# A graph-attention layer on one Trainium2 core: three late scores in one exponential, scores in batches of three and five, first loads spread

## The chip, the cores and the metric

The kernel runs on one core of a Trainium2 chip. The metric is the device time of one launch in microseconds. The engines are named as the profile names them: PE (matrix products, with PEld for its weight loads), DVE (vector), ACT (activation functions), POOL (GpSimd) and SP, whose queue issues most of the DMAs.

## The reference, cut to what matters

The network has four layers on 3327 nodes with 128 features and a dense 0/1 adjacency matrix. Each layer adds its output to x. Layer 1, an attention with 128 heads of size 8, takes nearly all the time, and all of the change is in it:

```python
h = jnp.maximum(_layernorm(x, axis=-1), 0.0)
q = (h @ Wq.T).reshape(d, n, 8)        # d = 128 heads, n = 3327 nodes
k = (h @ Wk.T).reshape(d, n, 8)
v = (h @ Wv.T).reshape(d, n, 8)
a = jnp.einsum('dnh,dmh->dnm', q, k) * d ** (-0.5)
a = a + adj + adj                       # twice the adjacency, the same for all heads
a = jax.nn.softmax(a, axis=2)
out = jnp.einsum('dnm,dmh->dnh', a, v).reshape(n, 8 * d) @ Wo.T
```

So for every head there is a 3327 x 3327 matrix of scores; twice the adjacency is added, the exponential is taken, and the result weighs the values. A ninth value column of ones gives the sum for the softmax.

## The kernel before, in words

Layer 0 runs first. Then comes a start stage (L458 to L478): for each of 26 row tiles r, PE makes q, k and v, ACT copies them out of PSUM (L466, L474), and SP stores them to DRAM (L440). Beside this, a list `early` (L444 to L457) holds pieces of other work, one of which is taken after each row: splitting q and k of the first groups into a high and a low part on POOL (`Parting`, L356), the loads of the first group (`load_heads`, L392), and rounding its keys (`key_pair`, L414). The exponentials of the adjacency for the first query chunk (`exp_of`, L345) are listed there too, though the program places them ahead of this stage on ACT. SP's queue runs in order, so a load that waits holds up the stores listed behind it.

The attention loop (L578 to L624) is written out by hand, and each engine takes its instructions in that order. There are 7 chunks of queries (six of 476 columns and one of 471, computed as 472), 32 groups of four heads, and 26 key tiles of 128 keys: 224 groups, and 2912 pairs of key tiles. One step is one key tile for four heads.

`scores` (L536) makes four products of a step, one head in each group of 32 rows of PE's array. Each of them ends up exponentiated in one of eight places of the tile `p8`, which a pair of steps shares. There are three ways, named in `WAYS` (L505):

- "D": the score goes to a one-bank PSUM tile `early` (four buffers), DVE adds the doubled adjacency `a2` (L552), and at the end of the pair one exponential on ACT covers the five D places (L557).
- "I": the score goes to a tile `late`, PE itself adds the doubled adjacency with the matrix `two_i` (L550), and ACT takes the exponential (L553).
- "G": the score goes to `late`, ACT takes the exponential (L553), and POOL multiplies by the exponential of the adjacency (L555).

An even step has D, D, D, I, an odd one D, D, I, G. So a pair has two L553 exponentials, of one score from a one-bank `late1` and of two scores from a two-bank `late2`, and one L557 of five scores. `weigh` (L559) multiplies the places of a step with the values and sums over the 26 key tiles in one PSUM bank `acc`; it runs four steps behind the scores. At a group's end DVE copies `acc` to `o4` (L573), and the next group's first values must wait for that copy. [...]

Of the kernel before, what the change touches and what calls it, by code (L numbers as in the profile page):

```python
# [8 lines left out]
F32 = mybir.dt.float32  # L9
# [6 lines left out]
AF = mybir.ActivationFunctionType  # L16
# [5 lines left out]
P = 128  # L22
# [32 lines left out]
def kernel(  # L55
# [285 lines left out]
    def even(c):  # L341
        w = q_chunks[c][1]
        return w + w % 2
# [45 lines left out]
                if t == 11:  # L389
                    self.store(side)  # L390

    def load_heads(c, g):  # L392
        q0, w = q_chunks[c]
        k_in = kq.tile([P, NP], F32, name="k_in", bufs=1)
        q4 = kq.tile([P, QW], F32R, name="q4")
        v4 = kq.tile([P, 4, T, EA], F32, name="v4")
        nc.gpsimd.memset(k_in[:, N:], 0.0)
        if w % 2:
            nc.gpsimd.memset(q4[:, w : w + 1].bitcast(F32), 0.0)
        for i in range(4):  # L400
            n0 = (4 * g + i) * N
            for j in range(2):
                r = 32 * i + HL * j
                nc.sync.dma_start(k_in[r : r + HL, :N], kt[:, n0 : n0 + N])
                nc.sync.dma_start(q4[r : r + HL, :w].bitcast(F32), dram(qt, E * j * GP + n0 + q0, [[0, 2], [GP, E], [1, w]]))
        for i in range(4):
            n0 = (4 * g + i) * N
            nc.sync.dma_start(
                v4[:, i].rearrange("p t e -> p (t e)"),
                vd[n0 : n0 + NP, :].rearrange("(p t) e -> p (t e)", t=T),  # L410
            )
        return k_in, q4, v4, []

    def key_pair(heads):  # L414
# [7 lines left out]
    with tc.tile_pool(name="l1", bufs=1) as pool, tc.tile_pool(name="l1_ps", bufs=3, space=PSUM) as ps:  # L422
        w_st = pool.tile([D, 3, NH * E], F32, name="w_st")
        for i, w in enumerate((wq, wk, wv)):
            nc.gpsimd.dma_start(w_st[:, i, :], w)
        zero = pool.tile([HL, NH], F32, name="zero")
        nc.vector.memset(zero, 0.0)
        nc.gpsimd.dma_start(vd[N * NH : N * NH + 1, :], zero[:1, :EA])
        for end in (qf, kf):
            nc.gpsimd.dma_start(end[:E, N * NH :], zero[:E])  # L430

        with tc.tile_pool(name="l1_ln", bufs=1) as ln, tc.tile_pool(name="l1_tp", bufs=2, space=PSUM) as tps:
            h, done = layernorm_relu(ln)
            done(T)
            hT = transposed(pool, tps, h, "hT")
        st = ctx_st.enter_context(tc.tile_pool(name="l1_st", bufs=4))

        def store(dst, src, r, kp):
            for p0, p1 in ((0, kp),) if kp == P else ((0, 112), (112, kp)):
                nc.sync.dma_start(dst[r * P + p0 : r * P + p1], src[p0:p1])  # L440


        assert 7 * N + NP <= 2 * P * NH
        early = []  # L444
        for g in range(2):
            part = Parting(g)
            for side in range(2):
                early.append(lambda part=part: (part.load(0), part.load(1)) if part.lo[0] is None else None)
                early.append(lambda part=part, side=side: [part.part(side, i) for i in range(4)] and part.store(side))
        first, e_first = [], []  # L450
        early.append(lambda: first.extend(load_heads(0, 0)))
        ahead_part = Parting(2)
        early.append(lambda: (ahead_part.load(0), ahead_part.load(1)))
        early.append(lambda: e_first.extend(exp_of(a, 0) for a in a_first[1::2]))
        early += [lambda: (key_pair(first), key_pair(first))] * (T // 4)
        if T // 2 % 2:
            early.append(lambda: key_pair(first))  # L457
        for r in range(T):  # L458
            kp = rows_of(r)
            lhs = hT[:, r * P : r * P + kp]  # L460
            for i, (dst, mx) in enumerate(((qf, q_max), (kf, k_max))):
                pp = ps.tile([P, 2, 512], F32, name="pp", bufs=2)
                for c in range(2):
                    nc.tensor.matmul(pp[:kp, c, :], lhs, w_st[:, i, c * 512 : c * 512 + 512], start=True, stop=True)
                s = st.tile([P, E * NH], F32, name="qk_st")
                nc.scalar.activation(s[:kp], pp[:kp].rearrange("p a b -> p (a b)"), AF.Copy, scale=D**-0.5 if i == 0 else 1.0)  # L466
                nc.vector.tensor_reduce(mx[:kp, r : r + 1], s[:kp], AX.X, ALU.max, apply_absolute_value=True)
                store(dst[:E].rearrange("e (r c) -> r e c", c=NH), s.rearrange("p (e c) -> p e c", c=NH), r, kp)
            pp = ps.tile([P, 2, 512], F32, name="pp", bufs=2)
            for c in range(2):  # L470
                nc.tensor.matmul(pp[:kp, c, :], lhs, w_st[:, 2, c * 512 : c * 512 + 512], start=True, stop=True)
            s = st.tile([P, NH, EA], F32, name="v_st")
            nc.gpsimd.memset(s[:, :, E : E + 1], 1.0)
            nc.scalar.copy(s[:kp, :, :E], pp[:kp].rearrange("p a (c e) -> p (a c) e", e=E))  # L474
            store(vd.rearrange("(r c) e -> r (c e)", c=NH), s.rearrange("p c e -> p (c e)"), r, kp)

            if r > 1 and early:
                early.pop(0)()  # L478
        while early:
            early.pop(0)()  # L480

        mx4 = pool.tile([P, 4], F32, name="mx4")
        for i, m in enumerate((q_max, k_max, a_max, low_bits)):
            nc.vector.tensor_reduce(mx4[:, i : i + 1], m, AX.X, ALU.max)
        all4 = pool.tile([P, 4], F32, name="all4")
        nc.gpsimd.partition_all_reduce(all4, mx4, P, bass_isa.ReduceOp.max)
        bound = pool.tile([P, 1], F32, name="bound")
        nc.vector.tensor_mul(bound, all4[:, 0:1], all4[:, 1:2])  # L490
        nc.vector.tensor_scalar_mul(bound, bound, 1.01 * E / 2)
        nc.vector.tensor_add(bound, bound, all4[:, 2:3])
        fits = pool.tile([P, 2], F32, name="fits")
        nc.vector.tensor_scalar(fits[:, 0:1], bound, SAFE / 2, None, op0=ALU.is_le)
        nc.vector.tensor_scalar(fits[:, 1:2], all4[:, 3:4], 0.0, None, op0=ALU.is_equal)
        nc.vector.tensor_mul(unsafe, fits[:, 0:1], fits[:, 1:2])
        nc.vector.tensor_scalar(unsafe, unsafe, -1.0, 1.0, op0=ALU.mult, op1=ALU.add)
        ctx_st.close()
# [3 lines left out]

    WAYS = ("DDDI", "DDIG")  # L505
    PLACES = ((0, 1, 2, 5), (3, 4, 6, 7))
    two_i = const.tile([P, P], BF16, name="two_i")
    nc.vector.tensor_copy(two_i, ident)
    engines = {
# [9 lines left out]
    with tc.tile_pool(name="at_in", bufs=1) as a_pool, tc.tile_pool(name="at_p", bufs=3) as p_pool, tc.tile_pool(  # L519
# [13 lines left out]
            q0, w = q_chunks[c]  # L533
            nc.sync.dma_start(adj16[t][:, q0 : q0 + w], a2[:, :w])

        def scores(step, heads, a2, e_a, p8):  # L536
            c, _, t = step
            we = even(c)
            _, q4, _, pairs = heads
            ways, places = WAYS[t % 2], PLACES[t % 2]  # L540
            n_d = ways.count("D")
            late = ps.tile([P, 4 - n_d, 512], F32, name=f"late{4 - n_d}")
            early = [ps.tile([P, 512], F32, name="early", bufs=4) for _ in range(n_d)]
            for i in (*range(n_d, 4), *range(n_d)):
                r = slice(32 * i, 32 * i + 32)
                sp = early[i] if i < n_d else late[:, i - n_d]
                nc.tensor.matmul(sp[:, :we], pairs[t // 2][r, t % 2, :], q4[r, :we], start=True, stop=ways[i] != "I")  # L547
            for i in range(4):
                if ways[i] == "I":
                    nc.tensor.matmul(late[:, i - n_d, :we], two_i, a2[:, :we], start=False, stop=True)  # L550
            for i in range(n_d):
                nc.vector.tensor_tensor(p8[:, places[i], :we], early[i][:, :we], a2[:, :we], op=ALU.add)  # L552
            nc.scalar.activation(p8[:, places[n_d] : places[3] + 1, :we], late[:, :, :we], AF.Exp)  # L553
            if ways[3] == "G":
                nc.gpsimd.tensor_tensor(p8[:, places[3], :we], p8[:, places[3], :we], e_a[:, :we], op=ALU.mult)  # L555
            if t % 2:
                nc.scalar.activation(p8[:, :5, :we], p8[:, :5, :we], AF.Exp)  # L557

        def weigh(step, v4, p8):  # L559
            c, g, t = step  # L560
# [17 lines left out]
        with tc.manual_schedule(engines=engines):  # L578
# [7 lines left out]
            for j, step in enumerate(steps):  # L586
# [6 lines left out]
                        a_t, a_next = a_next, []  # L593
                        e_t, e_next = e_next, []
                if t % 2 == 0:
                    p8 = p_pool.tile([P, 8, QW], F32, name="p8")
                scores(step, heads, a_t[t], e_t[t // 2], p8)
                begun[j] = (step, heads[2], p8)
                if j >= ahead:
                    weigh(*begun.pop(j - ahead))  # L600
                if t == min(4, T // 2) and more:
                    coming = load_heads(*groups[n])
                if c == 0 and g + 2 < n_groups:
# [506 lines left out]
```

## Time and profile before

| what | value |
|---|---|
| median of 3 runs | 11189.97 us (11184.46 to 11197.54) |
| profiled execution | 11195.14 us, of which 11193.4 us are the span from the first instruction to the last |
| busy in the span | PE 97%, ACT 91%, DVE 83%, POOL 54% |
| attention loop, first to last score product | 566.0 to 10468.7 us |
| PE clock granted | 0.989 of full speed over the span, 1.00 in the loop |

An engine's busy time counts the stretches in which at least one of its instructions runs. Instructions on one engine are pipelined and overlap, so the sum of their lengths is more than that, and a group's mean length is not the time that it holds the engine; the distance from one start to the next is. "idle before, releaser" says how long an engine stood before a group's instructions and which event ended the wait.

### The profile page before, as it was taken

Reading aid. Unit: us, or ns where it says so; the run is one execution under the profiler, and the core shown is the slowest. Engines: PE = TensorE matmul, PEld = TensorE weight load, DVE = VectorE, ACT = ScalarE, POOL = GpSimd, SP = SyncE. Lnnn points to the kernel's source line nnn. Section 1 sums busy time; section 2 is a strip of 40 time slices with the busy share of each in tenths; the row PEclk is TensorE's granted clock in tenths of the full one; section 3 lists DMA queues with packets and bytes.
Section 4 is the critical chain, followed back from the end, with each engine's and each line's share of the span. In section 5 each row is a group of like instructions: output and inputs, shape, how many; then the busy total and the mean of one; then the engine's idle time right before and its main releaser. Section 6 shows DMA issues by size and latency. Waiting matters only on the chain. (4 is left out here: it accounts for less than half of the span.)

```text
span 11193.4 us, 209350 instructions
## 1 busy us (share of the span) xinstructions
PE 10850.5 (97%) x79530; PEld 3005.9 (27%) x79530; DVE 9343.1 (83%) x15429; ACT 10199.3 (91%) x9152; POOL 6016.3 (54%) x6964
## 2 busy tenths in 40 slices
PE   9899999999999999999999999999999999999996
PEld 4322222222222222222222222222222222222453
DVE  8588888888888888888888888888888888888656
ACT  0399999999999999999999999999999999999522
POOL 0277777555555555555555555555555555555203
PEclk9899999999999999999999999999999999999998
DMA  7755554333333333333333333333333332333432
GB/s 264 238 129 120 123 127 109 65 64 64 68 64 62 67 66 63 68 65 61 68 66 63 66 66 61 67 66 61 66 66 61 66 63 55 61 58 58 135 113 97
DMA packets 417541, 942.25 MB, mean 84 GB/s; under 512 B 67936, under 2 KB 345937, under 8 KB 380940
## 3 DMA queue, kind: packets, MB, share of 16 engines
q1 hardware_dynamic: 412762, 918.98, 37.4%
q8 instruction: 627, 10.27, 0.4%
q0 software_dynamic: 3760, 9.78, 0.3%
q14 instruction: 392, 3.21, 0.1%
HBM read 788.78 MB, written 139.71 MB: 83 GB/s over the span
## 5 line engine op out<-in xcount | busy, mean ns | idle before, releaser
L552 DVE TENSOR_TENSOR p<-early,a 128x476 f32<-128x476 f32 (+1 forms) x14560 | 8426.4, 646 | 1369.4 <-PE early L547 1297.5
L557 ACT ACTIVATE p<-p 128x2380 f32<-128x2380 f32 (+1 forms) x2912 | 7568.4, 2599 | 0.4
L564 PE MATMUL acc<-p,v 128*9 128x476 f32 (+1 forms) x46592 | 5748.5, 564 | 15.3 <-ACT p L557 1.4
L553 ACT ACTIVATE p<-late 128x476 f32<-128x476 f32 (+1 forms) x5824 | 5315.4, 1175 | 13.8 <-DMA q<-qt 10.2
L555 POOL TENSOR_TENSOR p<-p,e 128x476 f32<-128x476 f32 (+1 forms) x2912 | 3528.1, 1212 | 3204.3 <-ACT p L553 2998.6
L547 PE MATMUL late<-q,k 32*128 32x476 f32 (+1 forms) x8736 | 2798.2, 478 | 99.5 <-ACT p L553 39.7
L547 PE MATMUL early<-q,k 32*128 32x476 f32 (+1 forms) x14560 | 2843.6, 478 | 9.4 <-DVE p L552 9.4
L419 POOL CAST k<-k_in 128x256 fp32r<-128x256 f32 x2912 | 1936.5, 697 | 886.4 <-DMA k_in<-kt 339.4
L547 PEld LDWEIGHTS late<-q,k 32*128 32x128 f32 x8736 | 1065.4, 181 | 4890.4 <-ACT p L553 4186.2
L550 PE MATMUL late<-a,two_i 128*128 128x476 bf16 (+1 forms) x5824 | 2180.8, 374 | 0.0
L547 PEld LDWEIGHTS early<-q,k 32*128 32x128 f32 x14560 | 1113.0, 181 | 9.9 <-DVE p L552 9.9
L564 PEld LDWEIGHTS acc<-p,v 128*9 128x9 f32 x46592 | 695.2, 88 | 1272.6 <-issue 1185.8
L550 PEld LDWEIGHTS <-two_i 128*128 128x128 bf16 x5824 | 556.2, 96 | 1329.0 <-issue 1329.0
L189 ACT COPY agg<-agg_ps 128x512 f32<-128x512 f32 x15 | 8.2, 591 | 485.5 <-PE agg_ps L204 290.6
L230 PE MATMUL agg_ps<-a,part 128*128 128x512 bf16 (+1 forms) x1092 | 227.0, 369 | 4.3 <-ACT agg L928 3.2
L272 POOL TENSOR_SCALAR a<-a_in 128x476 bf16<-128x476 f32 (+2 forms) x156 | 221.1, 1417 | 0.5
L272 POOL TENSOR_SCALAR a<-a 128x476 bf16<-128x476 f32 (+1 forms) x26 | 36.4, 1400 | 288.1 <-DMA a<-in_adjT_dram 288.1
L923 PE MATMUL sp<-yT,hT 128*128 128x512 f32 (+1 forms) x364 | 170.7, 610 | 12.3 <-ACT agg L928 6.4
L204 PE MATMUL agg_ps<-a,h 128*128 128x512 f32 (+2 forms) x364 | 148.2, 570 | 26.2 <-DVE h L164 26.2
L573 DVE COPY o<-acc 105x476 f32<-105x476 f32 (+1 forms) x224 | 144.5, 645 | 4.6 <-PE acc L564 4.6
L204 PE MATMUL agg_ps<-a,x 128*128 128x512 f32 (+2 forms) x364 | 145.3, 562 | 0.6 <-ACT x L318 0.6
L230 PEld LDWEIGHTS <-part 128*128 128x128 f16 x1092 | 108.6, 99 | 117.7 <-issue 10.3
(236 smaller groups left out, 2592.0 us busy)
## 6 DMA issues: line engine op xcount, KB each, us to landing
k_in<-kt SPq DMA_DIRECT2D x1792, 207.9 KB
v<-vd SPq DMA_DIRECT2D x896, 117.0 KB
a<-in_adjT_dram SPq DMA_DIRECT2D x50, 1663.5 KB
a<-adj SPq DMA_DIRECT2D x78, 831.8 KB
q<-qt SPq DMA_DIRECT2D x1536, 29.8 KB
a_in<-in_adjT_dram SPq DMA_DIRECT2D x125, 238.0 KB
adj<-a SPq DMA_DIRECT2D x156, 119.0 KB
vd<-v_st SPq DMA_DIRECT2D x25, 576.0 KB
```

Of the source, the lines that this page charges most:

```text
L204: nc.tensor.matmul(acc[c][:, :w], lhs[:kp, t, :], a[:kp, c0 : c0 + w], start=(t == 0), stop=(t == T - 1))
L230: nc.tensor.matmul(acc[c][:, :w], part[:, t, :], a[:, c0 : c0 + w], start=(t == 0 and i == 0), stop=(t == T - 1 and i == len(parts) - 1),)
L272: nc.gpsimd.tensor_scalar(a2[:kp, :w], a, 2.0, None, op0=ALU.mult)
L419: nc.gpsimd.tensor_copy(k, slots(k_in)[:, t : t + 2, :])
L547: nc.tensor.matmul(sp[:, :we], pairs[t // 2][r, t % 2, :], q4[r, :we], start=True, stop=ways[i] != "I")
L550: nc.tensor.matmul(late[:, i - n_d, :we], two_i, a2[:, :we], start=False, stop=True)
L552: nc.vector.tensor_tensor(p8[:, places[i], :we], early[i][:, :we], a2[:, :we], op=ALU.add)
L553: nc.scalar.activation(p8[:, places[n_d] : places[3] + 1, :we], late[:, :, :we], AF.Exp)
L555: nc.gpsimd.tensor_tensor(p8[:, places[3], :we], p8[:, places[3], :we], e_a[:, :we], op=ALU.mult)
L557: nc.scalar.activation(p8[:, :5, :we], p8[:, :5, :we], AF.Exp)
L564: nc.tensor.matmul(acc[32 * i : 32 * i + EA, :w], v4[:kp, i, t, :], p8[:kp, PLACES[t % 2][i], :w], start=(t == 0), stop=(t == T - 1),)
L923: nc.tensor.matmul(sp[:, c0 : c0 + w], slots(zT)[:, t, :], z2T[:, cols], start=True, stop=False)
```

## The change

Five edits, all in layer 1:

1. The three late scores of a pair (I of the even step, I and G of the odd one) go to one PSUM tile `late` of three banks with one buffer, and one exponential covers them. `scores` now treats a pair at once, at its even step.
2. The eight scores of a pair are made in two batches: first three of the even step's D scores, then five: the three late ones, then the odd step's two D scores. `BATCHES` lists them as (0 for even or 1 for odd, head). The two `two_i` products follow the second batch together.
3. Between the two batches stand the values of the even key tile of two pairs before; behind the second batch those of the odd one. The product with the exponential of the adjacency moves to `times_e`, at the odd step.
4. In the start stage the first group's loads are split into eight pieces: four with one head's keys and queries, one per row, then four with one head's values, each together with two roundings of keys. The load of the look-ahead parts comes ahead of them, and two empty entries of `early` are gone. The exponentials for the first chunk are listed with the roundings; on ACT they stand where they stood before.
5. The four buffers of `v_st` are made once, and their column of ones is set once instead of in every row.

```diff
-    def load_heads(c, g):
+    def load_heads(c, g, pieces=None):
...
-        for i in range(4):
+        def scored(i):
             n0 = (4 * g + i) * N
...
-        for i in range(4):
+        def weighted(i):
             n0 = (4 * g + i) * N
...
+        for f in (scored, weighted):
+            for i in range(4):
+                if pieces is None:
+                    f(i)
+                else:
+                    pieces.append(lambda f=f, i=i: f(i))
...
-                early.append(lambda part=part: (part.load(0), part.load(1)) if part.lo[0] is None else None)
+                if side == 0:
+                    early.append(lambda part=part: (part.load(0), part.load(1)))
...
-        early.append(lambda: first.extend(load_heads(0, 0)))
         ahead_part = Parting(2)
         early.append(lambda: (ahead_part.load(0), ahead_part.load(1)))
-        early.append(lambda: e_first.extend(exp_of(a, 0) for a in a_first[1::2]))
-        early += [lambda: (key_pair(first), key_pair(first))] * (T // 4)
+        pieces, e_first = [], []
+        first = load_heads(0, 0, pieces)
+        early += pieces[:4]
...
+                for f in pieces[4 + i : 5 + i if i < key_steps - 1 else None]:
+                    f()
+                for n in (2 * i, 2 * i + 1):
+                    if n < T // 2:
+                        key_pair(first)
+                        e_first.append(exp_of(a_first[2 * n + 1], 0))
...
-            s = st.tile([P, NH, EA], F32, name="v_st")
-            nc.gpsimd.memset(s[:, :, E : E + 1], 1.0)
+            s = v_sts[r % 4]
...
-    WAYS = ("DDDI", "DDIG")
-    PLACES = ((0, 1, 2, 5), (3, 4, 6, 7))
+    WAYS = ("IDDD", "DDIG")
+    PLACES = ((5, 0, 1, 2), (3, 4, 6, 7))
+
+    BATCHES = (((0, 1), (0, 2), (0, 3)), ((0, 0), (1, 2), (1, 3), (1, 1), (1, 0)))
...
+        def scores(step, heads, a2s, between):
...
+            p8 = p_pool.tile([P, 8, QW], F32, name="p8")
+            late = ps.tile([P, 3, 512], F32, name="late")
+            for n, batch in enumerate(BATCHES):
+                if n == 1:
+                    between()
+                for odd, i in batch:
+                    way, place = WAYS[odd][i], PLACES[odd][i]
+                    sp = ps.tile([P, 512], F32, name="early", bufs=4) if way == "D" else late[:, place - 5]
+                    r = slice(32 * i, 32 * i + 32)
+                    nc.tensor.matmul(sp[:, :we], pairs[t // 2][r, odd, :], q4[r, :we], start=True, stop=way != "I")
+                    if way == "D":
+                        nc.vector.tensor_tensor(p8[:, place, :we], sp[:, :we], a2s[odd][:, :we], op=ALU.add)
+            for odd, i in BATCHES[1]:
+                if WAYS[odd][i] == "I":
+                    nc.tensor.matmul(late[:, PLACES[odd][i] - 5, :we], two_i, a2s[odd][:, :we], start=False, stop=True)
+            nc.scalar.activation(p8[:, 5:, :we], late[:, :, :we], AF.Exp)
+            nc.scalar.activation(p8[:, :5, :we], p8[:, :5, :we], AF.Exp)
+            return p8
+
+        def times_e(step, p8, e_a):
+            we = even(step[0])
+            assert WAYS[1][3] == "G"
+            nc.gpsimd.tensor_tensor(p8[:, PLACES[1][3], :we], p8[:, PLACES[1][3], :we], e_a[:, :we], op=ALU.mult)
...
-                scores(step, heads, a_t[t], e_t[t // 2], p8)
+                    p8 = scores(step, heads, a_t[t : t + 2], lambda: weigh(*begun.pop(j - ahead)) if j >= ahead else None)
+                else:
+                    times_e(step, p8, e_t[t // 2])
+                    if j >= ahead:
+                        weigh(*begun.pop(j - ahead))
                 begun[j] = (step, heads[2], p8)
-                if j >= ahead:
-                    weigh(*begun.pop(j - ahead))
```

In the changed kernel the lines that matter are L575 (scores), L577 (DVE's add), L580 (identity products), L581 and L582 (the exponentials of three and of five scores), L588 (POOL's product), L595 (values), L604 (the copy of acc), L450 (stores), L406 and L407 (loads of keys and queries) and L411 (loads of values).

More of the change, by code (lines that the diff above doesn't have):

```diff
@@ L447, with step @@
             for side in range(2):
-                early.append(lambda part=part: (part.load(0), part.load(1)) if part.lo[0] is None else None)
+                if side == 0:
+                    early.append(lambda part=part: (part.load(0), part.load(1)))
                 early.append(lambda part=part, side=side: [part.part(side, i) for i in range(4)] and part.store(side))
-        first, e_first = [], []
-        early.append(lambda: first.extend(load_heads(0, 0)))
         ahead_part = Parting(2)
         early.append(lambda: (ahead_part.load(0), ahead_part.load(1)))
-        early.append(lambda: e_first.extend(exp_of(a, 0) for a in a_first[1::2]))
-        early += [lambda: (key_pair(first), key_pair(first))] * (T // 4)
-        if T // 2 % 2:
-            early.append(lambda: key_pair(first))
+        pieces, e_first = [], []
+        first = load_heads(0, 0, pieces)
+        early += pieces[:4]
+        key_steps = -(-(T // 2) // 2)
+        for i in range(key_steps):
+            def step(i=i):
+                for f in pieces[4 + i : 5 + i if i < key_steps - 1 else None]:
[4 more added lines that the diff above has]
+                        e_first.append(exp_of(a_first[2 * n + 1], 0))
+            early.append(step)
+        v_sts = [st.tile([P, NH, EA], F32, name=f"v_st{i}", bufs=1) for i in range(4)]
+        for s in v_sts:
+            nc.gpsimd.memset(s[:, :, E : E + 1], 1.0)
         for r in range(T):
@@ L534, in store_adj @@
             nc.sync.dma_start(adj16[t][:, q0 : q0 + w], a2[:, :w])
-        def scores(step, heads, a2, e_a, p8):
+        def scores(step, heads, a2s, between):
             c, _, t = step
@@ L539, in scores @@
             _, q4, _, pairs = heads
[L540 to L555, printed above, removed]
@@ L556, in scores @@
-            if t % 2:
-                nc.scalar.activation(p8[:, :5, :we], p8[:, :5, :we], AF.Exp)
+            p8 = p_pool.tile([P, 8, QW], F32, name="p8")
[10 more added lines that the diff above has]
+                        nc.vector.tensor_tensor(p8[:, place, :we], sp[:, :we], a2s[odd][:, :we], op=ALU.add)
@@ L595 @@
                 if t % 2 == 0:
-                    p8 = p_pool.tile([P, 8, QW], F32, name="p8")
-                scores(step, heads, a_t[t], e_t[t // 2], p8)
+                    p8 = scores(step, heads, a_t[t : t + 2], lambda: weigh(*begun.pop(j - ahead)) if j >= ahead else None)
[3 more added lines that the diff above has]
+                        weigh(*begun.pop(j - ahead))
                 begun[j] = (step, heads[2], p8)
-                if j >= ahead:
-                    weigh(*begun.pop(j - ahead))
                 if t == min(4, T // 2) and more:
```

## Prediction

> **What bounds the kernel now.** I read the page first: which engines are full, and which lines fill them.
>
> ```profile
> span 11193.4 us, 209350 instructions
> ...
> PE 10850.5 (97%) x79530; PEld 3005.9 (27%) x79530; DVE 9343.1 (83%) x15429; ACT 10199.3 (91%) x9152; POOL 6016.3 (54%) x6964
> ...
> L557 ACT ACTIVATE p<-p 128x2380 f32<-128x2380 f32 (+1 forms) x2912 | 7568.4, 2599 | 0.4
> L564 PE MATMUL acc<-p,v 128*9 128x476 f32 (+1 forms) x46592 | 5748.5, 564 | 15.3 <-ACT p L557 1.4
> L553 ACT ACTIVATE p<-late 128x476 f32<-128x476 f32 (+1 forms) x5824 | 5315.4, 1175 | 13.8 <-DMA q<-qt 10.2
> L230 PE MATMUL agg_ps<-a,part 128*128 128x512 bf16 (+1 forms) x1092 | 227.0, 369 | 4.3 <-ACT agg L928 3.2
> ```
>
> The attention loop runs from 566.0 us (first L547) to the last L547 at 10468.7, so 9903 us for 2912 pairs of key tiles: 3.401 us a pair. Both ACT and PE look full in it, so the page can't say which one sets the period. Durations overlap (one ACTIVATE drains while the next runs), so I went to the timeline and used distances between starts. Its columns are start, length, engine, line.
>
> ```profile
> 5001.26 2.55 ACT L557 ACTIVATE p<-p 128x2380 f32<-128x2380 f32 x1
> 5003.34 0.93 ACT L553 ACTIVATE p<-late 128x476 f32<-128x476 f32 x1
> 5003.78 1.34 ACT L553 ACTIVATE p<-late 128x952 f32<-128x952 f32 x1
> 5004.63 2.57 ACT L557 ACTIVATE p<-p 128x2380 f32<-128x2380 f32 x1
> ```
>
> ACT: the five-score exponential holds it for 2.08 us, the one-score one 0.45, the two-score one 0.85: 3.37 us a pair, with no gap. ACT sets the period. PE in the same stretch:
>
> ```profile
> 5002.76 0.48 PE L547 MATMUL early<-q,k 32*128 32x476 f32 x2
> 5003.18 0.37 PE L550 MATMUL late<-a,two_i 128*128 128x476 bf16 x1
> 5003.48 0.99 PE L564 MATMUL acc<-p,v 128*9 128x476 f32 x8
> 5004.40 0.48 PE L547 MATMUL late<-q,k 32*128 32x476 f32 x1
> ...
> 5007.86 0.64 DVE L573 COPY o<-acc 105x476 f32<-105x476 f32 x1
> ...
> 5008.55 0.12 PEld L564 LDWEIGHTS acc<-p,v 128*9 128x9 f32 x8 [0.34 <-DVE o L573]
> ```
>
> A key tile costs PE 0.42 us from its four scores to the identity product, 0.30 from there to the values, 0.92 from there to the next scores: 1.64, or 3.28 a pair. PE has only 0.09 us to spare against ACT's 3.37. That small margin decides this case. The last two lines are a group's end: the values of the next group wait until DVE has copied acc away.
>
> **What the skill says.** The Trainium skill, "ScalarE: Activation LUTs", section "What ACT_TABLE_LOAD costs", gives an ACTIVATE 186 ns plus 0.833 per element, of which neighbours overlap by about 93; a merged pair of instructions would save some 93 ns. The trace has one extra PSUM bank at 0.85 - 0.45 = 0.40 us, hence one bank's fixed part at about 0.05. I go by the trace: merging saves 0.05 us. The second is "TensorEngine Tiling (Array Packing)", section "Tiling Modes": changing the tiling mode drains the array. The trace agrees: 476 columns of a one-pass product in an unchanged mode take 0.20 us (L230: 227.0 us for 1092 products of 475 columns on average is 0.208; its 512-column ones start 0.216 apart), but identity to values takes 0.30, so a change of shape costs about 0.1.
>
> **The change part by part.**
>
> *One exponential for three late scores.* It removes 2912 ACTIVATEs. ACT a pair: 2.08 + 0.45 + 2 x 0.40 = 3.32 us instead of 3.37. If ACT stayed the bound this is 0.05 x 2912 = 146 us off.
>
> *Batches of three and five.* PE does the same 18 products, in another order: three scores, four values, five scores, both identities, four values. The four heads sit in four row groups and run at once; in the batch of five, head 0 occurs twice ((0,0) and (1,0)), so the fifth must follow the first in its own row group. That the scores are one pass I read from the last query chunk: 472 columns instead of 476 bring the identity about 2 ns nearer, as for the bf16 identity (2 ns), not 4 as one two-pass half of the values. So the fifth costs 0.20 us, if its weights load behind the running product. The two identities now stand together: the second costs 0.20 instead of 0.30 plus a change of mode. Scores straight to values do not occur before; nearest is scores to identity, 0.42, which I take (0.39 to 0.45). PE a pair: 0.42 + 0.92 + (0.42 + 0.20) + 0.20 + 0.30 + 0.92 = **3.38 us**, 0.10 more than its 3.28 now, and 0.06 over ACT's new 3.32. PE becomes the bound: 3.38 x 2912 = 9843 us; the last 416 pairs are about 0.025 us shorter (-10).
>
> *Waits inside a pair.* The late tile is now one buffer for all three. ACT is done with it about 1.74 us after its start (1.34 + 0.40); PE's next batch of five then needs 0.42 + 0.20 + 0.20 to start the second identity, 0.37 to finish, and some 0.13 for the two hand-overs: 3.06 us round, under 3.38, so it hides with 0.3 to spare. DVE's five adds are 0.56 apart, 2.8 us a pair; the last ends near 2.1 us after the batch of five starts, and ACT wants it at 2.5. The four early banks come free more than 0.4 us ahead. POOL's product with e has nearly two pairs until its values run. All cost nothing here.
>
> *Group ends, 224 of them.* Between the last values of a group and the first of the next lay scores and an identity (0.72 us); now only three scores (0.42). From the last values' second round (5007.18) to their end is 0.56, then the copy with its hand-overs 0.75; the next values may start 1.31 later at best, and PE would be there after 0.49 + 0.42 = 0.91. So 0.40 to 0.45 us stall, say 0.42 x 224 = 94 us, on the engine that is now the bound. In the kernel before the values lost 0.13 there, most of it absorbed.
>
> *Exponentials of the adjacency (L347)* inside the loop: 78, each 0.45 us of ACT. Before they add 35 us; afterwards ACT needs 3.77 in such a pair against 3.38, so 30.
>
> Loop: 9843 - 10 + 94 + 30 = 9957. The same sum for the kernel before (3.37 x 2912 = 9813, less 11, plus 35 and 23 for group ends) gives 9860, 43 short of the trace; I carry half of that, 21: 9978, or **+75 us**.
>
> *First loads spread.* SP's queue now puts the sixteen k_in and q loads between the stores of four rows, and the four v loads behind later ones; 22 POOL memsets that wait for a store of v_st go, and the look-ahead parts load earlier. Its place:
>
> ```profile
> 471.05 0.82 SPq L404 DMA_DIRECT2D k_in<-kt  x1
> ...
> 488.10 2.87 SPq L408 DMA_DIRECT2D v<-vd  x4
> ...
> 496.17 1.02 ACT L466 ACTIVATE qk_st<-pp 128x1024 f32<-128x1024 f32 x1 [18.07 <-DMA qf<-qk_st]
> ```
>
> The stores behind those loads wait, their four buffers fill and ACT stands 18 us. But the same bytes must go out and DMA is busy 0.85 of 376 to 566 us, full after 500, so part of the 18 returns as slower stores: 0 to 20, I take -12.
>
> Sum: 75 - 12 = +63 on the profiled execution of 11195.1 (span 11193.4), which is 5 above the median of 11190.0. So **11250 us**, 0.5% more.
>
> **Rivals.**
>
> *ACT stays the bound (faster).* The drain between scores and values, or the three-score burst, may be cheaper than 0.42, letting PE under 3.32. For it: ACT has been the bound, and the saving of 146 is sure. Against: the fifth score's 0.20 can't vanish, and PE had only 0.09 to spare. Full gain: 11190 - 146 - 12 + 10 for group ends = 11040. With PE at 3.35 instead of 3.38 it is 11250 - 87 = 11163.
>
> *The fifth score's weights are exposed (slower still).* If the load waits for the first score to leave row group 0, it adds 0.11 to 0.18 us (products with 128x128 f32 weights, L738, start 0.11 apart although such a load lasts 0.19): 0.11 x 2912 = 320, 11570. For it: no two scores in one row group run back to back in this trace. Against: in L564 the second four weight loads, in the same places as the first, are issued within 30 ns of them and the second round starts 0.40 later, with no gap.
>
> *The wait on the single late buffer decides.* It does once ACT's three-score exponential ends more than 0.3 us later than reckoned; each 0.1 beyond is 290 us. I see no reason.
>
> *It doesn't do what it says.* The order of instructions on PE and ACT of the changed program is as described, so no chance is kept for it.
>
> **How the numbers follow.** About 0.2% (22 us) is what a measurement of this kernel can tell from no change. PE-bound with a period of 3.36 to 3.42: 0.62, with its own range 11180 to 11370; exposed weights or a late-buffer wait: 0.13; ACT-bound or PE near it: 0.25. The first case reaches a little into "same". Faster 0.24, same 0.13, slower 0.63. Range 11080 to 11460: it takes in most of the faster case and half exposed weights.
>
> **What would show it.** Right: the five-score exponential's starts 3.38 apart within a group, ACT with gaps of 0.06, batch-of-five start to first identity 0.62, identities 0.20 apart, and a stall of about 0.42 of the values after each L604 copy. Wrong: ACT without gaps at 3.32 (faster), 0.75 or more from batch of five to identity (weights exposed), or that batch starting right after an ACT end with PE idle before it (late buffer). If the period is 3.38 but the whole is faster, the start stage gave more than 20 us.

## The result, and the profile after

The changed kernel takes 11285.06 us (median of 4 runs, 11283.75 to 11286.49) against 11189.22 us for the kernel before, measured beside it: a ratio of 1.0085, with a 95% interval of 1.0069 to 1.0101. It is slower by 96 us. The profiled execution took 11284.43 us.

The page of the changed kernel, the same parts as before:

```profile
span 11282.7 us, 206613 instructions
...
PE 10966.9 (97%) x79530; PEld 3044.0 (27%) x79530; DVE 9357.7 (83%) x15429; ACT 10188.2 (90%) x6240; POOL 6019.4 (53%) x6942
...
L582 ACT ACTIVATE p<-p 128x2380 f32<-128x2380 f32 (+1 forms) x2912 | 6348.7, 2180 | 0.0
L595 PE MATMUL acc<-p,v 128*9 128x476 f32 (+1 forms) x46592 | 5759.6, 564 | 86.6 <-DVE o L604 86.1
...
L581 ACT ACTIVATE p<-late 128x1428 f32<-128x1428 f32 (+1 forms) x2912 | 3967.2, 1362 | 125.1 <-PE late L580 118.6
```

ACT has 2912 instructions fewer and is busy 11 us less, in an execution that is 89 us longer. PE has the same number of products and is busy 116 us more. The idle columns changed sides: the exponential of the late scores (L581) now waits for PE's identity products (118.6 us), and the values (L595) wait for the copy of acc (86.1 us). In the kernel before, L553 stood idle for 13.8 us in all and the values for 15.3, of which the copy of acc made up 0.7. Nearly all of the new waiting lies at the ends of groups (212 of the 214 waits of L581, with 105 us, and 223 waits of the values, from the waits of each engine in the loop); 13.6 us are the loop's first pair. Inside a group ACT's short gaps don't show in this column, because its recorded lengths overlap.

The loop, from the start of the first L575 to that of the last, runs from 556.7 to 10558.8 us: 10002.1 us, where it took 9902.6. The start stage is 9.4 us shorter, what follows the loop 0.8 us shorter. So +99.5 - 9.4 - 0.8 = +89.3 us, the difference of the spans.

Two more views show where the 100 us lie. First the timeline within a group (start, length, engine, line):

```profile
5002.02 2.18 ACT L582 ACTIVATE p<-p 128x2380 f32<-128x2380 f32 x1
...
5002.83 0.48 PE L575 MATMUL late<-q,k 32*128 32x476 f32 x3
5002.84 0.69 PE L575 MATMUL early<-q,k 32*128 32x476 f32 x2
5003.46 0.57 PE L580 MATMUL late<-a,two_i 128*128 128x476 bf16 x2
5003.97 0.98 PE L595 MATMUL acc<-p,v 128*9 128x476 f32 x8
5004.15 1.36 ACT L581 ACTIVATE p<-late 128x1428 f32<-128x1428 f32 x1
5004.88 0.48 PE L575 MATMUL early<-q,k 32*128 32x476 f32 x3
5005.30 0.99 PE L595 MATMUL acc<-p,v 128*9 128x476 f32 x8
5005.41 2.18 ACT L582 ACTIVATE p<-p 128x2380 f32<-128x2380 f32 x1
...
5006.21 0.48 PE L575 MATMUL late<-q,k 32*128 32x476 f32 x3
```

PE goes from the batch of five to the identities in 0.63 us, to the values in 0.51, to the batch of three in 0.91, to the next values in 0.42, and 0.91 later starts the next batch of five: 3.38 here, 3.383 in the median of the pairs with 476 columns, with nothing in between. ACT's five-score exponentials stand 3.39 apart, and between one of them and the late one lie 2.13 us instead of the 2.08 that it holds ACT. PE sets the period.

Is that longer than before? The prediction read ACT's need in the kernel before from the starts of its instructions, 3.37 us a pair. The lengths say something else. In its two lines of L557 the starts are 3.37 us apart, but the second exponential is 0.02 longer (2.57 against 2.55), so the ends are 3.39 apart. Over the whole loop the ends of L557 are 3.387 us apart in the median, at each of the 13 places that a pair can have in its group. The starts are 3.369 apart from the third to the sixth pair of a group, where the lengths grow from 2.60 to 2.67 us, and 3.383 to 3.386 from the eighth to the twelfth, where the lengths stay at 2.68. So ACT's starts can run ahead of its ends for a while, and over a whole group it is the ends that count. Inside a group the changed kernel's 3.383 us is not longer than the 3.387 before: PE took back what the merge freed on ACT, and no more. The 100 us lie elsewhere.

Second, the same at a group's end:

```profile
4997.56 0.49 PE L575 MATMUL early<-q,k 32*128 32x476 f32 x3
...
4997.72 0.66 DVE L604 COPY o<-acc 105x476 f32<-105x476 f32 x1
...
4998.43 0.22 PEld L595 LDWEIGHTS acc<-p,v 128*9 128x9 f32 x8 [0.69 <-DVE o L604]
4998.43 1.08 PE L595 MATMUL acc<-p,v 128*9 128x476 f32 x8 [0.38 <-DVE o L604]
...
4999.44 0.49 PE L575 MATMUL late<-q,k 32*128 32x476 f32 x3
```

From the batch of three to the values it is 0.87 us instead of 0.42, because these are the first values of the next group and acc is still being copied. Then they take 1.01 instead of 0.92 to the next scores: their eight weight loads last 0.22 us together here, against 0.12 elsewhere. From one five-score exponential to the next, the pair with a group's end is 3.913 us long on average, 0.53 more than the median of 3.383. In the kernel before that pair is as long as the others (3.398 us on average, both). So the group ends add 224 x 0.53 = 119 us, more than the whole loss of the loop; the shorter pairs give back 2912 x 0.004 = 12 us, and smaller things make up the difference to 99.5.

### The profile page after: what moved, and what is told of

Same layout as the page of the kernel before. It is cut to its first block, busy times and chain, and to the rows that moved or that the text cites. A ratio compares the mean times of both kernels' runs of the same rounds, so it can differ in the third digit from the quotient of the medians.

```text
span 11282.7 us, 206613 instructions
## 1 busy us (share of the span) xinstructions
PE 10966.9 (97%) x79530; PEld 3044.0 (27%) x79530; DVE 9357.7 (83%) x15429; ACT 10188.2 (90%) x6240; POOL 6019.4 (53%) x6942
## 5 line engine op out<-in xcount | busy, mean ns | idle before, releaser
L577 DVE TENSOR_TENSOR p<-early,a 128x476 f32<-128x476 f32 (+1 forms) x14560 | 8421.4, 644 | 1442.3 <-PE early L575 1365.0
L582 ACT ACTIVATE p<-p 128x2380 f32<-128x2380 f32 (+1 forms) x2912 | 6348.7, 2180 | 0.0
L595 PE MATMUL acc<-p,v 128*9 128x476 f32 (+1 forms) x46592 | 5759.6, 564 | 86.6 <-DVE o L604 86.1
L588 POOL TENSOR_TENSOR p<-p,e 128x476 f32<-128x476 f32 (+1 forms) x2912 | 3528.5, 1212 | 3350.1 <-ACT p L581 3328.8
L581 ACT ACTIVATE p<-late 128x1428 f32<-128x1428 f32 (+1 forms) x2912 | 3967.2, 1362 | 125.1 <-PE late L580 118.6
L575 PE MATMUL early<-q,k 32*128 32x476 f32 (+1 forms) x14560 | 3413.7, 457 | 11.9 <-DVE p L577 10.8
L575 PEld LDWEIGHTS early<-q,k 32*128 32x128 f32 x14560 | 1372.4, 182 | 2334.6 <-DVE p L577 2329.5
L580 PE MATMUL late<-a,two_i 128*128 128x476 bf16 (+1 forms) x5824 | 1674.7, 369 | 0.0
L575 PE MATMUL late<-q,k 32*128 32x476 f32 (+1 forms) x8736 | 1415.6, 479 | 22.7 <-ACT p L581 22.5
L595 PEld LDWEIGHTS acc<-p,v 128*9 128x9 f32 x46592 | 715.2, 88 | 1917.0 <-issue 1762.1
L575 PEld LDWEIGHTS late<-q,k 32*128 32x128 f32 x8736 | 547.3, 181 | 2345.9 <-ACT p L581 2176.3
L580 PEld LDWEIGHTS <-two_i 128*128 128x128 bf16 x5824 | 330.7, 97 | 964.8 <-issue 964.8
L604 DVE COPY o<-acc 105x476 f32<-105x476 f32 (+1 forms) x224 | 146.3, 653 | 15.8 <-PE acc L595 7.3
```

The source lines that it names most:

```text
L575: nc.tensor.matmul(sp[:, :we], pairs[t // 2][r, odd, :], q4[r, :we], start=True, stop=way != "I")
L577: nc.vector.tensor_tensor(p8[:, place, :we], sp[:, :we], a2s[odd][:, :we], op=ALU.add)
L580: nc.tensor.matmul(late[:, PLACES[odd][i] - 5, :we], two_i, a2s[odd][:, :we], start=False, stop=True)
L581: nc.scalar.activation(p8[:, 5:, :we], late[:, :, :we], AF.Exp)
L588: nc.gpsimd.tensor_tensor(p8[:, PLACES[1][3], :we], p8[:, PLACES[1][3], :we], e_a[:, :we], op=ALU.mult)
L595: nc.tensor.matmul(acc[32 * i : 32 * i + EA, :w], v4[:kp, i, t, :], p8[:kp, PLACES[t % 2][i], :w], start=(t == 0), stop=(t == T - 1),)
```

## The experiments

Theory: PE is the bound of the changed kernel, by the fifth score of the second batch and the copy at group ends. Rivals: the drains between batches, the single late buffer, or ACT. Where a ratio stands, it is to runs of the kernel before that were made beside it (medians of 11192.7 us for e1 and e2, 11193.1 for e5 and e6). e3, e4 and e7 ran once each and are set against the changed kernel's 11285.06; their differences of 91 us and more stand far above the 4 us by which the medians of the kernel before differ.

**Batches of four and four (e1).** One head in each row group.

```diff
-    BATCHES = (((0, 1), (0, 2), (0, 3)), ((0, 0), (1, 2), (1, 3), (1, 1), (1, 0)))
+    BATCHES = (((0, 1), (0, 2), (0, 3), (1, 0)), ((0, 0), (1, 2), (1, 3), (1, 1)))
```

> The batches are four and four, with one head in each row group: (0,1), (0,2), (0,3), (1,0), then (0,0), (1,2), (1,3), (1,1). Nothing else is changed. Theory (PE is the bound of the changed kernel, and the fifth score, alone in its row group, costs it 0.21 us a pair): PE needs 0.42 + 0.92 + 0.42 + 0.21 + 0.29 + 0.92 = 3.18 us a pair, ACT 3.32, so ACT sets the period again; with the fourth early bank coming free a little late the pairs are 3.32 to 3.36 us apart, the group-end stall is mostly absorbed, and the kernel takes 11090 to 11180 us, less than the kernel before. Rival (the loss comes from the drains between batches, or from the single late buffer): the period stays near 3.38 and the time between 11240 and 11300.

Measured: 11203.34 us, ratio 1.0009 (1.0003 to 1.0016). That is between the two expectations. The fifth score did cost what was said: second batch to identity is 0.42 us again instead of 0.63, and the loss of 0.85% shrinks to 0.09%. The order of batches, and so of the array's changes of shape, is the same as in the changed kernel, and so is the single late buffer; neither is what cost the 0.21. But the gain of the merged exponential didn't come out. The timeline of a pair of this kernel shows what stands in its place:

```profile
5018.69 0.64 DVE L577 TENSOR_TENSOR p<-early,a 128x476 f32<-128x476 f32 x1
5019.00 0.19 PEld L575 LDWEIGHTS early<-q,k 32*128 32x128 f32 x3 [0.80 <-DVE p L577]
...
5019.39 0.18 PEld L575 LDWEIGHTS early<-q,k 32*128 32x128 f32 x1 [0.20 <-DVE p L577]
...
5019.80 0.12 PEld L595 LDWEIGHTS acc<-p,v 128*9 128x9 f32 x8 [0.23 <-issue]
```

The first three scores of the batch start at 5019.00, the fourth only at 5019.39: it needs the fourth early bank, and DVE's last add of the pair before, which ends at 5019.33, has to free it. Every second pair pays this, so that the five-score exponentials stand 3.32 and 3.41 us apart in turn (medians), 3.37 on average. The short pairs show that ACT can do with 3.32; the bank, which I had called "a little late", takes most of that gain. The group ends, which I expected to be mostly absorbed, still cost 0.35 us each (3.72 against 3.37), and they take the rest: in means the pairs inside a group last 3.379 us where the kernel before has 3.398, a gain of 52 us over 2688 pairs, and the 224 pairs at group ends 3.716, a loss of 71. So the loop is 20 us longer than before, and the shorter start stage gives back 9.

**Two exponentials again (e2).** The changed kernel, but with ACT's old division.

```diff
-            nc.scalar.activation(p8[:, 5:, :we], late[:, :, :we], AF.Exp)
+            nc.scalar.activation(p8[:, 5:6, :we], late[:, :1, :we], AF.Exp)
+            nc.scalar.activation(p8[:, 6:, :we], late[:, 1:, :we], AF.Exp)
```

> As the changed kernel, but the late tile is read by two exponentials again, one of one score and one of two. Theory (PE is the bound at 3.383 us a pair): ACT goes from 3.32 to 3.37 a pair, still under PE, so the time stays within 25 us of the changed kernel's (11285 to 11310). Rival (the merged exponential is earning its 0.05 us a pair, and something else costs more): 2912 x 0.05 = 146 us slower, about 11430.

Measured: 11291.25 us, ratio 1.0090 (1.0072 to 1.0108); the changed kernel had 1.0085. The merge is worth 6 us here, not 146, and the intervals don't tell even that from nothing. ACT's timeline in this kernel:

```profile
5005.57 2.19 ACT L583 ACTIVATE p<-p 128x2380 f32<-128x2380 f32 x1
5007.65 0.57 ACT L581 ACTIVATE p<-late 128x476 f32<-128x476 f32 x1
5008.11 0.96 ACT L582 ACTIVATE p<-late 128x952 f32<-128x952 f32 x1
5008.95 2.19 ACT L583 ACTIVATE p<-p 128x2380 f32<-128x2380 f32 x1
```

From start to start that is 2.08 + 0.46 + 0.84 = 3.38 us, PE's period; from end to end it is 3.386 in the median, ACT's need of before. So ACT with its old division just keeps up with PE, and with the merge it has some 0.06 us to spare that the changed kernel can't use. ACT is not what makes it slow.

**The fifth score twice (e3).**

```diff
                     nc.tensor.matmul(sp[:, :we], pairs[t // 2][r, odd, :], q4[r, :we], start=True, stop=way != "I")
+                    if (odd, i) == (1, 0):
+                        nc.tensor.matmul(sp[:, :we], pairs[t // 2][r, odd, :], q4[r, :we], start=True, stop=True)
```

> As the changed kernel, but the score (1,0) is made twice in a row into the same bank, so that the second batch has six products, three of them in row group 0. Theory: one more product in the same row group and mode costs PE its 0.20 to 0.21 us, all of it on the path: 2912 x 0.205 = 597 us more, about 11880, with 0.83 us from the batch's start to the first identity instead of 0.63. Rival (PE has slack, and ACT or the late buffer is the bound): less than 200 us more.

Measured: 11898.3 us in one run, 613 more than the changed kernel. PE's timeline:

```profile
5006.06 0.48 PE L575 MATMUL late<-q,k 32*128 32x476 f32 x3
5006.07 0.68 PE L575 MATMUL early<-q,k 32*128 32x476 f32 x2
5006.59 0.38 PE L577 MATMUL early<-q,k 32*128 32x476 f32 x1
5006.90 0.58 PE L582 MATMUL late<-a,two_i 128*128 128x476 bf16 x2
```

Batch to identity is 0.84 us, 0.22 more than with five (0.63; 0.844 against 0.628 in the medians), and 613 / 2912 = 0.21 a pair: one more product in an occupied row group goes onto the path in full, and PE has no slack.

**The copy of acc twice (e4).**

```diff
                 nc.vector.tensor_copy(o4[: 96 + EA, :w], acc[: 96 + EA, :w])
+                nc.vector.tensor_copy(o4[: 96 + EA, :w], acc[: 96 + EA, :w])
```

> As the changed kernel, but DVE copies acc to o4 twice at each group's end. Theory (the next group's first values wait for the copy on the engine that is the bound): each second copy takes DVE 0.56 us and all of it reaches PE: 224 x 0.56 = 126 us more, about 11410, and the stall of the values after the copy grows from 0.55 to about 1.1 us. Rival (the group-end wait is absorbed by slack elsewhere): at most 40 us more.

Measured: 11441.45 us in one run, 156 more, or 0.70 us a group. DVE's timeline:

```profile
5022.02 0.65 DVE L604 COPY o<-acc 105x476 f32<-105x476 f32 x1
5022.71 0.65 DVE L605 COPY o<-acc 105x476 f32<-105x476 f32 x1
```

The second copy starts 0.69 us after the first, not the 0.56 that I took from DVE's adds; with that, the sum fits (224 x 0.69 = 155). All of it reaches PE. An add starts 0.57 us after the copy ahead of it (median), so it isn't the copy as such that takes 0.69: the second one starts 0.04 after the end of the first, whose tile it writes again.

**Three copies of four left out (e7).**

```diff
-                o4 = a_pool.tile([P, QW], F32, name="o4")
-                nc.vector.tensor_copy(o4[: 96 + EA, :w], acc[: 96 + EA, :w])
+                if g % 4 == 0:
+                    o4_now[:] = [a_pool.tile([P, QW], F32, name="o4")]
+                    nc.vector.tensor_copy(o4_now[0][: 96 + EA, :w], acc[: 96 + EA, :w])
+                o4 = o4_now[0]
```

> The changed kernel with the copy of acc left out in three groups of four (168 of 224), so most of the attention's output is stale. It takes away the wait itself. Theory (0.45 us of stall and 0.10 us of weights loaded late at each group's end, all on PE's path): 168 x 0.53 = 89 us less, about 11196. Rival (something else at a group's end, the late keys or values, holds PE as well): less than 40 us less.

Measured: 11194.27 us in one run, 91 less than the changed kernel. So a group's end is worth 91 / 168 = 0.54 us. Pairs at a group's end now last 3.385 us in the median (three of four have no copy), as others do, so the copy is what held PE there.

**The start stage alone (e5).** The loop of the kernel before, with edits 4 and 5.

> The kernel before with edits 4 and 5 alone (start stage); its attention loop is that of before. The loop of the changed kernel began 9.4 us earlier (556.7 against 566.0 us). Theory (that comes from the start stage alone, and the loop adds its own +100): the loop begins near 557 us and the time is 9 us (0.08%) below the kernel before, about 11180. Rival (the earlier start is given back at the loop's beginning, where the first groups' loads are late): no difference.

Measured: 11184.42 us against 11193.09, ratio 0.9992 (0.9984 to 1.0000). The loop begins at 558.3 us instead of 566.0. What the stage does with DMA stands in the windows from 376 to 557 us (busy time and number of instructions for PE, PEld, DVE, ACT and POOL, then PE's clock, DMA share, GB/s), first of the kernel before, then of this run:

```profile
376.00:557.00 181.00, 146.91 (x307) 63.12 (x308) 61.45 (x52) 79.31 (x82) 33.57 (x71) 0.87 0.84 253
```

```profile
376.00:557.00 181.00, 154.60 (x325) 65.72 (x325) 65.97 (x57) 83.98 (x86) 26.59 (x49) 0.90 0.89 268
```

The DMA engines are busy 0.89 of the time instead of 0.84. This part is a gain of 9 us at the edge of what is measurable, and the best of the kernels run. Edits 4 and 5 were not tried apart, so which of them brings it is open; that fuller DMA engines are the cause fits the windows, and is not shown by itself.

**Four and four with two exponentials (e6).** The edits of e1 and e2 together.

> Batches of four and four as in the run with that name, but the late tile is read by two exponentials, of one and of two scores. There PE has slack, so ACT counts. Theory (the merged exponential is worth its 0.05 us a pair wherever PE is not the bound): pairs 0.03 to 0.05 us longer than with one exponential, 90 to 146 us more, 11290 to 11350. Rival (with four and four the early bank that comes free late is the bound, not ACT): less than 40 us more.

Measured: 11208.33 us, ratio 1.0014 (1.0007 to 1.0020), some 5 us more than e1. The number is the rival's, its reason is not. ACT's timeline:

```profile
5021.60 2.22 ACT L583 ACTIVATE p<-p 128x2380 f32<-128x2380 f32 x1
5023.67 0.60 ACT L581 ACTIVATE p<-late 128x476 f32<-128x476 f32 x1
5024.12 1.00 ACT L582 ACTIVATE p<-late 128x952 f32<-128x952 f32 x1
5024.96 2.24 ACT L583 ACTIVATE p<-p 128x2380 f32<-128x2380 f32 x1
```

The starts inside a group are 3.368 us apart (median), as close as in the kernel before where they are closest, and ACT waits for PE for 4.6 us in the whole loop. So here ACT sets the pace inside a group, and the bank does in e1. The ends are 3.386 apart, against 3.365 on average in e1: the merge does save 0.021 us in such a pair, 56 us in all. At the group ends it is lost again. There the ends are 3.500 us apart in e6, 0.11 more than elsewhere, in e1 they are 3.729 apart, 0.36 more: 224 x 0.25 = 56 us. I read this as a backlog of ACT's that it works off while PE stands at the copy, and that the merge takes away. No kernel run here shows the 0.05 us of the merge as time saved in the whole.

## Why the prediction was right, point by point

The mechanism was right in the changed kernel: PE takes over as the bound. Its time a pair was put at 3.38 us, and the median is 3.383. The terms (medians of the trace): three scores to values 0.417 (taken as 0.42), second batch to identity 0.628 (0.62), identity to identity 0.211 (0.20), identity to values 0.294 (0.30), values to scores 0.916 twice (0.92). Undoing the batch of five (e1) and doubling its last score (e3) show that the fifth score is what brings PE there. That the merge spares ACT 0.05 us, and not the other estimate of some 93 ns, is borne out by starts: 3.318 us in e1's short pairs, 3.368 in e6. The rival of exposed weights is out: the fifth and the sixth score cost 0.21 and 0.22, close to one pass. The rival of ACT as the bound is out by e2.

What was wrong is the other side of the comparison. ACT's need in the kernel before was read from starts as 3.37 us, and is 3.387 by ends. So the term of the period, 9843 against 9813 us, was put at 30 us more where the runs have 12 less. The sum for the kernel before fell 43 us short of its trace for that reason in the main: 2912 x 0.017 = 50, with 10 for a stop in the loop's first pair (PE waits 9.4 us for DVE there, and 10.8 in the changed kernel), less the 23 for group ends, which cost nothing. Carrying half of the 43 over, 21, had no reason behind it, and took 22 of the 30 us away again; that the sum came so near is luck in this part.

The late buffer hides, as said. The round that I put at 3.06 us is shorter still, as the late exponential lasts 1.36 us and not 1.74; outside group ends the batch of five follows the values after 0.918 us or less in 97 of 100 pairs, with no wait.

The step that was too small is the group's end: 0.42 us and 94 us in the sum, where the trace has 0.53 and 119. And they are the whole loss: 94 - 23 = 71 us more than before were forecast for them, 119 came. The stall itself is 0.455, just above my 0.40 to 0.45; left out were 0.10 us that the values themselves take longer after the wait (1.014 against 0.916 in the medians), as their weight loads are stretched from 0.12 to 0.22 us. Where e7 has no copy, the values take 0.916 again. But it isn't the wait alone: in the kernel before, these loads wait for the copy too (0.34 us in the prediction's last line of PEld) and last 0.12. There the identity product stands ahead of them, here three scores. Why that matters stays open.

The exponentials of the adjacency and the remainder carried over, 30 + 21, came to 43: the loop of 10002 less 2912 x 3.383 = 9851, plus 11 for the narrow chunk, less 119. Some 27 of it are the pairs with such an exponential, and about 10 the stop in the first pair.

The start stage gave 9.4 us instead of 12, and e5 shows that it lasts to the end.

In all: 11258 forecast for the profiled execution, 11284 measured. Of the 26 us, 25 are the group ends; the other terms cancel. The profiled execution lies 1 us below its median now, where the one before lay 5 above; that and rounding are the other 9 us between 11250 and 11285.

## What to carry to other kernels

Where two engines are within 3% of each other, an edit that frees one of them must be priced on the other: 0.05 us saved on ACT cost 0.10 on PE, since the batches of three and five fit the row groups badly. Count products by row group, not by number: five scores over four row groups are two rounds. And where a buffer is handed over at a group's end, ask how much work lies between its last use and its next one; moving 0.3 us of it elsewhere turned a wait that cost nothing into half a microsecond, 224 times. And where an engine has no gaps, compare its ends as well as its starts: if the lengths grow from one round to the next, the starts understate what it needs.

With the same eight PSUM banks (four early, three late, acc), the runs show three orders that meet three limits at nearly the same time: ACT (before, 3.387 us), PE (three and five, 3.383), and inside a group the early bank (four and four, 3.365).

## What the runs showed of the hardware that was not expected

The recorded length of an ACTIVATE is not what it costs, and the distance of starts is not always either. The five-score exponential has a mean of 2599 ns in the kernel before and 2180 ns in the changed one, and yet the next exponential can start 2.08 us after it in both (in the changed one, where it needn't wait for PE); a one-score exponential from PSUM lasts 0.93 us before and 0.57 us in e2. In the kernel before, where ACT never waits, the lengths are the longer ones. In e6, after a group's end has let ACT catch up, they grow by 0.018 us from pair to pair, from 2.19 to 2.41 us over a group: starts 3.368 apart, ends 3.386. In the kernel before they stop growing at 2.68 us, and from there on the starts too are 3.385 apart. What holds the ends back is not shown.

Two DVE copies into the same tile start 0.69 us apart (e4), while adds into different places of a tile start 0.56 us apart, and an add follows a copy after 0.57.
